# Layer 0's banded query operand in scratch padded to 32 rows and loaded once per unit; FFN heads and the second unit's load moved ahead of layer 1's weight products

## The chip, the cores and the metric

The kernel runs on one core of a Trainium2 chip. The metric is the device time of one execution in microseconds (us), here the median over several runs of the same program. The engines are TensorE (PE, with its weight loads as PEld), VectorE (DVE), ScalarE (ACT), GpSimd (POOL) and SyncE (SP), which issues most of the DMAs. Each engine works through its own list of instructions in order and waits on semaphores for the others. DMAs are put on a queue by SP or ACT and carried out by 16 DMA engines.

## The reference, cut to what matters

The input is x, 16 batches of 512 tokens with 128 features. Two layers of "macaron" form follow each other: half an FFN, attention, half an FFN. Layer 1 has a mixture of experts in its FFN and a linear attention; the change touches only weight products of it that are made ahead. What the change is about is layer 0:

```python
x = x + 0.5 * L0_ffn(layernorm(x))          # fp4_linear: blocks of 16, quantised and scaled back
x = x + L0_attn(layernorm(x))
x = x + 0.5 * L0_ffn(layernorm(x))
...
# L0_attn, 16 heads of 8 features:
idx  = arange(s); dist = clip(idx[None, :] - idx[:, None], -64, 64) + 64
pe_k = rel_emb_k[dist]; pe_v = rel_emb_v[dist]
score = einsum('bhqd,bhkd->bhqk', q, k) + einsum('bhqd,qkd->bhqk', q, pe_k)
attn  = softmax(score)
ctx   = einsum('bhqk,bhkd->bhqd', attn, v) + einsum('bhqk,qkd->bhqd', attn, pe_v)
```

The second term of the score depends on the distance of query and key. Outside a band around the diagonal the distance is clipped, and the term is a constant per query and side; inside the band it needs a matmul of its own.

## The kernel before, in words

**Units.** Layer 0 works in units: unit u = 2b + half is one half (256 queries) of batch b, for all 16 heads. A unit has two passes over its scores. The first, `maxima`, makes 32 score tiles of 128 keys by 512 columns, takes the running maximum of each on DVE (`mx`, L341), and ends with `mn`, the negated maximum of every query and head (L352), which goes by way of DRAM (`MD`, L353) into row 28 of each group of the tile `BD` (L355). The second, `main`, makes the same 32 tiles again, now with the maximum taken off by the matmul itself, exponentiates them on ACT (`PT`, L369) and multiplies by the values.

**One score tile** (`scores`). Four matmuls take keys `KS` against `BD` (L263). If the tile touches the band, eight more take `ET`, shifted rows of the relative key embeddings, against `TQ`, the queries arranged by head and distance (L267). The contraction runs over 128 rows, in four groups of 32 of which 24 are used by `TQ`.

**From queries to BD and TQ.** `prep(b)` normalises the batch, multiplies by the q and k weights, and splits the results into two f16 parts (`qkhi`, `qklo`). The k part and the q part go to the DRAM scratches `KSd` and `QS` (L302), some bias rows to `QS` as well (L309). For the band, the q parts are spread into `HM`, a tile that is zero except for its own head's rows, and twelve DMAs of 128 KB write it to the DRAM scratch `QM` (L300): on ACT's queue for batch 0, on SP's for the others. `loadK(b)` brings KS back in eight DMAs (L315), `load(b, half)` brings BD in four (29 rows, 58 KB each, L329) and TQ in four (24 rows each, L330; again on ACT's queue for batch 0). BD and TQ have three buffers, used by turns by the units. Their unused rows are zeroed once, TQ's on POOL, BD's on DVE.

**FFN steps.** `head(b, h)` is the first FFN of half a batch, `tail(b, h)` the second, each 21 steps of normalising, quantising, two products and a third one. `head` of a new batch begins with the load of x (L476), and DVE's first step on it is `ln_st` (L55). A tail ends with the store of x to DRAM (X, L487), which frees the x buffer for a later load.

**Order.** `layer0` writes the order out in a prologue and then hands over to `interleave`, which takes steps from the units' generators by due times: `main` of a unit runs beside `maxima` of the next, `head` three batches ahead and `prep` two batches ahead. On top of this a scheduler of the language places instructions on each engine by its own estimates, so that the order on an engine follows the program's text only loosely. The prologue before the change, where `pA` and `wp` are pools:

```python
            run(prep(0)); run(prepV(0)); loads(0); run(mxs(0,0))
            FFN1.pre(s,wp,[...],w)
        big=c.enter_context(tc.tile_pool(name="big",bufs=3))
        loads(1); ffn2(head,1); run(prep(1)); run(part(14)); ffn2(head,2)
```

`FFN1.pre` prepares layer 1's expert weights: for each of eight experts it loads w1 and w2 (L567), transposes w1 on PE (L568), multiplies and stores the product `We`. `Attn0.__init__` sets up layer 0's constants: `padv` and `hk` (L205, L207) for the values' embeddings, `padk` and `ET` for the keys', the zero row of QS (`zr`, L244), and four fills of KS on ACT (L236). The FFN's constructor quantises its weights and transposes them (L98) before head 0 can multiply.

Of the kernel before, what the change touches and what calls it, by code (L numbers as in the profile page):

```python
# [9 lines left out]
F16 = mybir.dt.float16  # L10
# [131 lines left out]
def f16split(nc, src, hi, lo, eng_lo):  # L142
    nc.vector.tensor_copy(hi,src)
    eng_lo.tensor_tensor(lo,src,hi,ALU.subtract)

class Attn0:

    def __init__(a, s, wk, pp, wqkv, bqkv, wout, bout, rek, rev):
        nc=s.nc; a.s=s; a.nc=nc
        c=s.const; dr=s.dram  # L150
# [70 lines left out]
        a.KS=[c.tile([128,2,2048],F16,name=f"a0_KS{i}") for i in range(2)]  # L221
        a.V=[c.tile([128,6,168],F32,name=f"a0_V{i}") for i in range(2)]
        a.cr=[c.tile([128,1024],F32,name=f"a0_cr{i}") for i in range(1)]
        for i in range(3): nc.vector.memset(a.BD[i],0.0); nc.gpsimd.memset(a.TQ[i],0.0)
        for t in a.V:
            nc.gpsimd.memset(t[:,:,144:168],0.0)
            nc.gpsimd.memset(t[:,:,0:144].rearrange("p w (h c) -> p w h c",c=9)[:,:,:,8:9],1.0)
# [8 lines left out]
            for sd in range(2): nc.scalar.activation(t[:,sd,:],a.BD[2].rearrange("p g h q -> p (g h q)")[:,0:2048],AF.Identity,bias=rm[:,sd:sd+1])  # L236
        zr=wk.tile([16,512],F16,name="zr"); nc.vector.memset(zr,0.0)
        a.QS=[dr.tile([16,29,512],F16,name=f"QS{i}") for i in range(2)]
        a.QM=[dr.tile([4,16,24,512],F16,name=f"QM{i}") for i in range(2)]
        a.KSd=[dr.tile([16,24,512],F16,name=f"KSd{i}") for i in range(2)]  # L240
        a.MD=[dr.tile([16,256],F16,name=f"MD{i}") for i in range(2)]
        a.X=4*8*1024+1024
# [32 lines left out]
    def prep(a, b, xb, wk, pM):  # L275
        s=a.s; nc=a.nc
        i=b%2
        QS=a.QS[i]; KSd=a.KSd[i]
        xn=wk.tile([128,4,128],F32,name="xn")
        yield from s.ln_steps(xb,xn,wk,4)  # L280
        ps=pM.tile([128,512],F32,name="mps")
        for j in range(4): nc.tensor.transpose(ps[:,j*128:(j+1)*128],xn[:,j,:],a.ident)
        xnT=a.xnT[b]=wk.tile([128,512],F32,name="xnT",bufs=2); nc.scalar.copy(xnT,ps); yield
        for z in range(2):
            ps=pM.tile([128,512],F32,name="mps")
            nc.tensor.matmul(ps,a.w[:,z*128:(z+1)*128],xnT,start=True,stop=True)
            f=wk.tile([128,512],F32,name="qk0") if z==0 else wk.tile([128,4,128],F32,name="xn").rearrange("p a b -> p (a b)")
            if z==0:
                for hf in range(2):
                    c=slice(hf*256,hf*256+256)  # L290
                    nc.scalar.activation(f[:,c].rearrange("p (b x j) -> p b j x",j=4,x=8),ps[:,c].rearrange("p (b j x) -> p b j x",j=4,x=8),AF.Identity,bias=a.bq[:,0:1],scale=float(1/np.sqrt(8.0)))
                q=f
            else: nc.scalar.activation(f,ps,AF.Identity,bias=a.bq[:,1:2])
            hi=wk.tile([128,512],F16,name="qkhi",bufs=2); lo=wk.tile([128,512],F16,name="qklo")
            f16split(nc,f,hi,lo,nc.gpsimd)
            if z==0:
                for t,e,m in ((hi,nc.vector,a.HM[0]),(lo,nc.gpsimd,a.HM[1])):
                    e.tensor_copy(bass.AP(tensor=m.tensor,offset=m.offset,ap=[m.ap[0],[513,4],[4,128]]),t.rearrange("p (y j) -> p j y",j=4))
                for p,t in enumerate((a.HM[0],a.HM[1],a.HM[0])):
                    for j in range(4): (nc.sync if b else nc.scalar).dma_start(a.QM[i][j][:,p*8:p*8+8,:],t[:,j,:])  # L300
            for p,t in enumerate((hi,lo,hi) if z==0 else (hi,hi,lo)):
                nc.sync.dma_start((QS,KSd)[z][:,p*8:p*8+8,:],t)  # L302
            yield
        ps=pM.tile([128,512],F32,name="mps")
        nc.tensor.matmul(ps[:32],a.eb.rearrange("p a b -> p (a b)"),q,start=True,stop=True)
        rhi=wk.tile([128,512],F16,name="qkhi",bufs=2)[:32]; rlo=wk.tile([128,512],F16,name="qklo")[:32]
        nc.vector.tensor_copy(rhi,ps[:32]); nc.vector.tensor_tensor(rlo,ps[:32],rhi,ALU.subtract)
        for sd in range(2):
            nc.sync.dma_start(QS[:,24+2*sd,:],rhi[16*sd:16*sd+16]); nc.sync.dma_start(QS[:,25+2*sd,:],rlo[16*sd:16*sd+16])  # L309
        yield  # L310
# [14 lines left out]
    def load(a, b, half):  # L325
        nc=a.nc; i=b%2
        u=(2*b+half)%3; BD=a.BD[u]; TQ=a.TQ[u]; QS=a.QS[i]
        for j in range(4):
            nc.sync.dma_start(BD[j*32:j*32+29,:,j,:],QS.rearrange("(g j) r q -> j r g q",j=4)[j][:,:,half*256:half*256+256])  # L329
            (nc.sync if b else nc.scalar).dma_start(TQ[j*32:j*32+24],a.QM[i][j][:,:,half*256:half*256+256].rearrange("h r q -> r h q"))  # L330

    def maxima(a, b, half, wk, pS, pM):

# [113 lines left out]
def interleave(*gens):  # L447

    live=[[g,n,0,f,t] for g,n,f,t in (q if len(q)==4 else (*q,0,1) for q in gens)]
    while live:  # L450
        k=min(live,key=lambda r:r[3]+(r[4]-r[3])*r[2]/r[1])
        try: next(k[0]); k[2]+=1
        except StopIteration: live.remove(k)
# [4 lines left out]
def layer0(tc, s, w, src, dst, nb=16):  # L458
    nc=tc.nc
    tok=lambda x,b: x[b].rearrange("(t p) d -> p t d",p=128)  # L460
    P="L0_attn_"; names=["W_qkv","b_qkv","W_out","b_out","rel_emb_k","rel_emb_v"]
    with ExitStack() as c:
        s.const=c.enter_context(tc.tile_pool(name="c",bufs=1))
        pM=c.enter_context(tc.tile_pool(name="pM",bufs=2,space=PS))
        pF=c.enter_context(tc.tile_pool(name="pF",bufs=0,space=PS)) if 0 else pM
        pS=c.enter_context(tc.tile_pool(name="pS",bufs=3,space=PS))
        pX=pS
        pA=c.enter_context(tc.tile_pool(name="pA",bufs=1,space=PS))
        wk=c.enter_context(tc.tile_pool(name="wk",bufs=1))
        fk=c.enter_context(tc.tile_pool(name="fk",bufs=2))  # L470
        xk=c.enter_context(tc.tile_pool(name="xk",bufs=5))
        X={}
        def xload(b):
            if b in X or b>=nb: return
            t=xk.tile([128,4,128],F32,name="x"); X[b]=t
            nc.sync.dma_start(t,tok(src,b))  # L476
        def head(b,h):

            if b<nb: xload(b); yield from F.half(X[b],h,fk,pF)
        def prep(b):  # L480
            if b<nb: yield from A.prep(b,X[b],wk,pM)
        def prepV(b):
            if b<nb: yield from A.prepV(b,pM)
        def tail(b,h):
            if b<0: return
            yield from F.half(X[b],h,fk,pF)
            nc.sync.dma_start(tok(dst,b)[:,2*h:2*h+2,:],X[b][:,2*h:2*h+2,:])  # L487
        def mxs(b,half):
            if b>=nb: return
            yield from A.maxima(b,half,wk,pX,pM)  # L490
        def loads(u):
            if u<2*nb:
                if u%2==0: A.loadK(u//2)
                A.load(u//2,u%2)
        def stream():
            for u in range(1,2*nb):
                for k,_ in enumerate(mxs(u//2,u%2)):
                    if k==16: loads(u+1)
                    yield
        st=stream()  # L500
        def part(n):
            for _ in range(n):
                if next(st,0)==0: return
                yield
        pl,hl=2,3
        W=dict(part=0,V=(.6,.7),fin=(.45,.9),prep=(0,.7),tail=1.0,head=(-.1,1))
        with tc.tile_pool(name="wp",bufs=1) as wp:
            for b in range(3): xload(b)
            F=FFN(s,w["L0_ffn_w_gate"],w["L0_ffn_w_up"],w["L0_ffn_w_down"],wp,pF)
            ffn2=lambda f,b: interleave((f(b,0),21,0,.8),(f(b,1),21,.2,1))  # L510
            ffn2(head,0)
            A=Attn0(s,wp,pS,*[w[P+n] for n in names])
            def run(g):
                for _ in g: pass
            run(prep(0)); run(prepV(0)); loads(0); run(mxs(0,0))
            FFN1.pre(s,wp,[pA.tile([128,512],F32,name=f"av{z}") for z in range(2)]+[pA.tile([128,512],F32,name="rps")],w)
        big=c.enter_context(tc.tile_pool(name="big",bufs=3))
        loads(1); ffn2(head,1); run(prep(1)); run(part(14)); ffn2(head,2)
        S=[(part(99999),33*2*nb,W['part'],2*nb+W['part'])]
        for b in range(nb):  # L520
            for h in range(2):
                u=2*b+h
                def at(g,n,f,t): S.append((g,n,u+f,u+t))
                at(A.main(b,h,X,wk,big,pS,pA,pM),59,0,1)
                fn,tl=(W['fin'],W['tail']) if u<2*nb-2 else ((.3,.5),.6)
                at(A.fin(b,h,X,wk,pM),5,1+fn[0],1+fn[1])
                at(tail(b,h),21,1+fn[1]+.001,1+fn[1]+tl)
                if b+hl<nb: at(head(b+hl,h),21,*W['head'])
                if h==0 and b+pl<nb: at(prep(b+pl),11,*W['prep'])
                if h==1 and b+1<nb: at(prepV(b+1),1,*W['V'])  # L530
        interleave(*S)
# [507 lines left out]
```

## Time and profile before

| | before |
|---|---|
| median of 3 runs | 3653.02 us (3648.55 to 3656.99) |
| the profiled execution | 3669.38 us, span 3667.4 us |
| mean granted TensorE clock | 0.90 |
| busy PE / DVE / ACT / POOL | 2895.4 / 2453.7 / 1702.8 / 839.6 us |
| first QS write issued | 86.15 us |
| first score matmul | 124.3 us |
| MD of units 0, 1, 2, 3 issued | 164.5, 219.9, 284.8, 345.1 us |
| layer 0 ends, about | 2095 us |

The times of the three runs and the profiled execution are of the same program; the profiled one was 16.4 us above the median. "Idle before, releaser" and the waits name what an engine stood waiting for, inferred from semaphores. The granted clock is the share of TensorE's full clock that it was allowed, and the DMA share is the mean over 16 DMA engines.

### The profile page before, as it was taken

To read this page: it belongs to the slowest core of one execution; us is meant where nothing else is said; L and a number is where in the kernel's file an instruction comes from. 1 tells how busy PE (TensorE), PEld (TensorE's weight loads), DVE (VectorE), ACT (ScalarE), POOL (GpSimd) and SP (SyncE) were. 2 spreads that over 40 slices of the span, in tenths; PEclk is the share of its full clock that TensorE was granted. 3 is DMA by queue.
4 is the path that set the end of the run, shared out by engine and by line. 5 is a ranking of instruction groups with operands and counts; after the bars stand their busy time and mean duration, and the time that the engine had idled before them with its cause. 6 is when DMAs were issued, how large, how long until landed. Compare 5 with 4: busy or idle time off the path is not lost. (4 is left out here: it accounts for less than half of the span.)

```text
span 3667.4 us, 95252 instructions
## 1 busy us (share of the span) xinstructions
PE 2895.4 (79%) x40077; PEld 2076.7 (57%) x40077; DVE 2453.7 (67%) x6508; ACT 1702.8 (46%) x3391; POOL 839.6 (23%) x789
## 2 busy tenths in 40 slices
PE   5579888898988989899988278882688888878570
PEld 3357666777767776677776144441465555555340
DVE  5568678777877788777764457774546656545357
ACT  3145445544554545545545155542455455445242
POOL 4122122222222222222101222222112121111226
PEclk8789999999999999999999588885899999999785
DMA  3232122322232122322210101104322222121301
GB/s 109 52 86 70 46 63 59 78 64 47 55 78 71 45 63 64 77 63 45 68 38 20 40 24 35 38 30 110 90 73 58 59 65 67 36 61 36 123 19 46
DMA packets 290159, 217.23 MB, mean 59 GB/s; under 512 B 77402, under 2 KB 257476, under 8 KB 289604
## 3 DMA queue, kind: packets, MB, share of 16 engines
q1 hardware_dynamic: 284468, 207.72, 21.5%
q8 instruction: 315, 5.16, 0.6%
q10 hardware_dynamic: 5264, 3.43, 0.4%
q14 instruction: 112, 0.92, 0.1%
HBM read 110.28 MB, written 100.78 MB: 58 GB/s over the span
## 5 line engine op out<-in xcount | busy, mean ns | idle before, releaser
L341 DVE TRANSPOSE_TENSOR_REDUCE mx<-sps 128x16 f32<-128x512 f32 x1024 | 706.0, 701 | 262.3 <-PE sps L267 138.6
L263 PE MATMUL sps<-a_BD,a_KS 128*128 128x128 f16 x8192 | 745.5, 222 | 156.2 <-DVE mx L341 96.2
L369 ACT ACTIVATE PT<-sps 128x512 f32<-128x512 f32 x1024 | 580.4, 598 | 554.0 <-PE sps L267 289.1
L263 PEld LDWEIGHTS <-a_KS 128*128 128x128 f16 x8192 | 540.3, 98 | 309.2 <-issue 257.7
L59 POOL TENSOR_TENSOR ln_rs<-ln_ve,negh 128x4 f32<-128x4 f32 (+1 forms) x192 | 175.3, 921 | 857.1 <-DVE ln_ve L58 778.3
L267 PE MATMUL sps<-a_TQ,a_ET 128*128 128x64 f16 x7168 | 370.2, 194 | 0.3 <-issue 0.3
L722 DVE SCALAR_TENSOR_TENSOR moe<-mps,oh,moe 128x128 f32<-128x128 f32 x896 | 289.8, 341 | 112.7 <-PE mps L720 99.7
L79 POOL TENSOR_TENSOR q_M<-q_y,q_M 128x704 f32<-128x704 f32 (+2 forms) x129 | 159.2, 1235 | 862.4 <-DVE q_y L78 650.7
L720 PE MATMUL mps<-f_W,T 128*128 128x512 f32 x512 | 302.9, 714 | 17.9 <-DVE moe L722 13.6
L267 PEld LDWEIGHTS <-a_ET 128*128 128x128 f16 x7168 | 309.8, 99 | 6.9 <-issue 6.5
L274 PE MATMUL av<-PT,a_V 128*32 128x256 f32 x3840 | 251.4, 386 | 0.0
L895 DVE TENSOR_TENSOR a_at<-pp,a_cm 128x1024 f32<-128x1024 f32 x128 | 154.4, 1215 | 71.7 <-PE pp L893 71.0
L274 PE MATMUL rps<-PT,a_TV 128*32 128x64 f32 x6912 | 199.5, 225 | 0.1
L893 PE MATMUL pp<-a_F 64*128 64x128 f32 x2048 | 165.1, 300 | 37.6 <-DVE a_at L895 29.9
L893 PEld LDWEIGHTS pp<-a_F 64*128 64x128 f32 x2048 | 139.3, 201 | 84.1 <-DVE a_at L895 36.0
L720 PEld LDWEIGHTS mps<-f_W,T 128*128 128x128 f32 x512 | 104.4, 227 | 118.5 <-issue 75.0
L274 PEld LDWEIGHTS av<-PT,a_V 128*32 128x32 f32 x3840 | 135.4, 111 | 55.8 <-issue 1.9
L274 PEld LDWEIGHTS rps<-PT,a_TV 128*32 128x32 f32 x6912 | 129.7, 110 | 50.1 <-issue 26.1
L875 ACT ACTIVATE a_F<-pp 128x1024 f32<-128x1024 f32 x128 | 127.0, 1027 | 45.5 <-PE pp L873 30.5
L62 ACT ACTIVATE xn<-xn,ln_mr,ln_rs 128x128 f32<-128x128 f32 x256 | 103.7, 483 | 87.8 <-DVE ln_mr L60 44.3
L139 PE MATMUL mps<-wdT,hT 128*128 128x128 f32 (+1 forms) x768 | 134.0, 313 | 7.6 <-ACT hT L136 7.3
L674 ACT COPY f_PT<-St 32x512 f32<-32x512 f32 x128 | 78.7, 615 | 105.4 <-DVE St L673 101.3
(342 smaller groups left out, 5338.3 us busy)
## 6 DMA issues: line engine op xcount, KB each, us to landing
QM<-a_HM SPq DMA_DIRECT2D x180, 128.0 KB
a_TQ<-QM SPq DMA_DIRECT2D x120, 192.0 KB
RD<-RV SPq DMA_DIRECT2D x32, 512.0 KB
a_KS<-KSd SPq DMA_DIRECT2D x128, 96.0 KB
a_QK<-a1d SPq DMA_DIRECT2D x128, 96.0 KB
xn<-X SPq DMA_DIRECT2D x32, 256.0 KB
a1d<-a_hi SPq DMA_DIRECT2D x64, 128.0 KB
a_BD<-QS SPq DMA_DIRECT2D x128, 58.0 KB
```

The costliest lines, as they stand in the source:

```text
L59: nc.gpsimd.tensor_tensor(rs,ve,s.negh[:,:n],ALU.pow); yield
L79: nc.gpsimd.tensor_tensor(M[:P],y[:P],M[:P],ALU.subtract)
L139: nc.tensor.matmul(ps[:,384:512],hT[:P,c,:],f.wdT[:P,c,:],start=(c==0),stop=(c==2),skip_group_check=True)
L263: nc.tensor.matmul(o4[:,g],KS[:,sd,g*512+kt*128:g*512+(kt+1)*128],BD[:,g,:,b*32:b*32+32].rearrange("p h (x j) -> p x h j",j=4),start=(g==0 ...
L267: nc.tensor.matmul(out[:,x*64:x*64+64],a.ET[:,w0:w0+128],TQ[:,:,b*32+4*x:b*32+4*x+4],start=False,stop=(x==7),skip_group_check=True)
L274: for p,q in mms[1:]: a.nc.tensor.matmul(*p,**q)
L341: r=nc.vector.tensor_reduce(mx[:,kt,:,bb],ps.rearrange("p (i c) -> p i c",c=32),axis=AX.X,op=ALU.max,apply_transpose=True)
L369: nc.scalar.activation(pt[:,:,bb*32:bb*32+32].rearrange("p h (x j) -> p x h j",j=4),ps.rearrange("p (x h j) -> p x h j",x=8,j=4),AF.Exp)
L720: nc.tensor.matmul(ps,yT[:,j*128:(j+1)*128],a.W[:,e2*4:e2*4+4,:],start=True,stop=True)
L722: nc.vector.scalar_tensor_tensor(moe[:,j,:],ps[:,e*128:(e+1)*128],oh[:,j,e2*4+e:e2*4+e+1],moe[:,j,:],ALU.mult,ALU.add)
L893: nc.tensor.matmul(ps[:,hh,bs],f[hh*64:hh*64+64,1,bs],f[hh*64:hh*64+64,0,bs],start=True,stop=True)
L895: nc.vector.tensor_tensor(k,ps.rearrange("p h (b q) -> p (h b) q",b=4),a.cm.unsqueeze(1).to_broadcast([128,8,128]),ALU.mult)
```

## The change

The scratch QM is laid out anew: by half of the batch, by group, then 32 rows (24 of data and 8 that stay zero), heads and 256 queries, so that a unit's TQ tile lies in DRAM as it stands in SBUF, 128 rows of 8 KB. Sixteen DMAs in the setup write the zero rows, from HM while it is all zero. The three memsets of TQ on POOL go. Each batch writes QM in 24 DMAs of 64 KB instead of 12 of 128 KB, behind the QS writes in the text and on SP's queue for every batch, and `load` fetches TQ in one DMA of 1 MB instead of four of 192 KB, on SP for every batch, ahead of BD's four. In `layer0`, the line with the second unit's loads, head 1, prep 1, fourteen steps of maxima and head 2 moves in front of `FFN1.pre`, into the block of the pool `wp`.

```diff
-        for i in range(3): nc.vector.memset(a.BD[i],0.0); nc.gpsimd.memset(a.TQ[i],0.0)
+        for i in range(3): nc.vector.memset(a.BD[i],0.0)
...
-        a.QM=[dr.tile([4,16,24,512],F16,name=f"QM{i}") for i in range(2)]
+        a.QM=[dr.tile([2,4,32,16,256],F16,name=f"QM{i}") for i in range(2)]
+        for i,t in enumerate(a.QM):
+            for k in range(8): nc.sync.dma_start(t[k//4,k%4,24:32].rearrange("r (c h) q -> (r c) (h q)",c=2),a.HM[i].rearrange("p j q -> p (j q)")[k*16:k*16+16])
...
-                for p,t in enumerate((a.HM[0],a.HM[1],a.HM[0])):
-                    for j in range(4): (nc.sync if b else nc.scalar).dma_start(a.QM[i][j][:,p*8:p*8+8,:],t[:,j,:])
             for p,t in enumerate((hi,lo,hi) if z==0 else (hi,hi,lo)):
                 nc.sync.dma_start((QS,KSd)[z][:,p*8:p*8+8,:],t)
+            if z==0:
+                for hf in range(2):
+                    for p,t in enumerate((a.HM[0],a.HM[1],a.HM[0])):
+                        for j in range(4): nc.sync.dma_start(a.QM[i][hf,j,p*8:p*8+8].rearrange("r h q -> h r q"),t[:,j,hf*256:hf*256+256])
...
+        nc.sync.dma_start(TQ,a.QM[i][half].rearrange("j r h q -> (j r) h q"))
         for j in range(4):
             nc.sync.dma_start(BD[j*32:j*32+29,:,j,:],QS.rearrange("(g j) r q -> j r g q",j=4)[j][:,:,half*256:half*256+256])
-            (nc.sync if b else nc.scalar).dma_start(TQ[j*32:j*32+24],a.QM[i][j][:,:,half*256:half*256+256].rearrange("h r q -> r h q"))
...
-            run(prep(0)); run(prepV(0)); loads(0); run(mxs(0,0))
+            run(prep(0)); run(prepV(0)); loads(0); run(mxs(0,0)); loads(1); ffn2(head,1); run(prep(1)); run(part(14)); ffn2(head,2)
             FFN1.pre(s,wp,[pA.tile([128,512],F32,name=f"av{z}") for z in range(2)]+[pA.tile([128,512],F32,name="rps")],w)
         big=c.enter_context(tc.tile_pool(name="big",bufs=3))
-        loads(1); ffn2(head,1); run(prep(1)); run(part(14)); ffn2(head,2)
```

## The prediction

> **What bounds the kernel now.** First the page: TensorE is busiest, and layer 0's two big consumers are the score matmuls and VectorE's running maxima.
>
> ```profile
> PE 2895.4 (79%) x40077; PEld 2076.7 (57%) x40077; DVE 2453.7 (67%) x6508; ACT 1702.8 (46%) x3391; POOL 839.6 (23%) x789
> ...
> L341 DVE TRANSPOSE_TENSOR_REDUCE mx<-sps 128x16 f32<-128x512 f32 x1024 | 706.0, 701 | 262.3 <-PE sps L267 138.6
> ...
> QM<-a_HM SPq DMA_DIRECT2D x180, 128.0 KB
> a_TQ<-QM SPq DMA_DIRECT2D x120, 192.0 KB
> ...
> a_BD<-QS SPq DMA_DIRECT2D x128, 58.0 KB
> ```
>
> An average says nothing of the prologue, so next the table by stretches, cut at the first QS write (86.15), the first score (124.3) and the issue of MD (the negated maxima) of units 0 to 3. Columns: start and end, length, busy PE, PEld, DVE, ACT, POOL, then granted clock, DMA share, GB/s.
>
> ```profile
> 86.15:124.30 38.15, 6.17 (x16) 2.57 (x17) 5.22 (x8) 1.52 (x3) 4.15 (x3) 0.54 0.56 132
> 124.30:164.50 40.20, 29.19 (x309) 24.05 (x310) 37.82 (x85) 5.55 (x16) 10.35 (x10) 0.77 0.02 7
> 164.50:219.90 55.40, 44.23 (x724) 32.84 (x721) 40.80 (x82) 20.97 (x46) 11.75 (x10) 0.95 0.33 79
> 219.90:284.80 64.90, 51.71 (x784) 38.84 (x785) 40.22 (x82) 30.55 (x64) 13.68 (x13) 0.88 0.26 65
> 284.80:345.10 60.30, 56.36 (x1040) 43.56 (x1033) 48.38 (x109) 30.57 (x68) 16.73 (x16) 1.00 0.31 84
> 345.10:2095.00 1749.90, 1520.24 (x26261) 1196.83 (x26259) 1301.35 (x2886) 853.20 (x1855) 382.55 (x363) 0.95 0.23 57
> ```
>
> For 38 us nearly everything stands (PE 6.17, DVE 5.22); in the next 40 us DVE is full (37.82 of 40.20). The waits between 86.15 and 220 say why (total, times, longest):
>
> ```profile
> PE sps L263 <- DMA a_BD<-QS: 20.2, 2, 15.7
> ACT f_x L116 <- DMA a_TQ<-QM: 18.6, 1, 18.6
> DVE mx L341 <- PE sps L267: 21.5, 4, 16.2
> ```
>
> The first scores wait for BD. ACT, which issues batch 0's QM writes and TQ loads itself, cannot start head 1's copy f_x for 18.6 us, and head 1 then shares DVE with the first maxima. Last, the waits of the steady part, 330 to 2050:
>
> ```profile
> PE sps L263 <- DVE mx L341: 75.6, 107, 4.6
> ...
> DVE ln_st L55 <- DMA x<-in_L_attn_x_dram: 43.4, 11, 8.0
> ...
> PE sps L263 <- DMA a_BD<-MD: 0.6, 1, 0.6
> ```
>
> PE works 1520 of those 1720 us. It never waits for MD's way back; but DVE waits for the x load in eleven batches, and PE's own gaps around these waits add up to 36.8 us. So x is on the path, MD has room.
>
> **Setup (up to the first QS write).** The three TQ memsets leave POOL: 10.4 us between 5.7 and 16.1, in which one small DVE step took 2.40 us instead of 0.19. ACT's four KS fills move to the front, so the quantised-weight transposes (40.59) can start about 2 us earlier. Against it SP gets 16 pad writes of 64 KB between padv and hk. The trace has none; the nearest rows, writes of 16 rows, take 0.30 to 0.56 us to issue, a QM write 0.61: 5 to 10 us of SP, mostly while it waited for work. Pushed back: hk (issued 25.86) and the first w1t (19.28 to about 34). The weight products then no longer stand ahead of the quantised-weight transposes but among head 0's steps: the instruction order has about one expert there instead of five. I put the first QS write at 84, between 81 and 91.
>
> **First QS write to first score: 38.2 us before.** Queue SP, in the new order: QS x3, QM x24, KSd x3, QS rows, TQ, KS x8, BD x4. Before, batch 0's 12 QM writes and 8 TQ loads ran on ACT's queue beside it; so here all of the QM time is new in SP's line. A QM write took 0.61 to 0.65 us with 128 rows; the new ones have 128 rows too, of half the size, so I take the same: the second batch, which had its 12 on SP already, needed 39.3 us from QS to landed BD. From that: +12 x 0.65 = +7.8. TQ becomes one issue instead of three in front of BD (-2.0), and a 1.2 us wait for a qklo write is covered: about 43. The 1 MB TQ load (128 rows of 8 KB) has hk as its row: packets of 342 to 367 ns, 8 for each of 16 engines, 2.9 us, against 8 TQ loads before (3072 packets of 42 ns, 8 us of all engines) which shared the engines with the KS loads; the KS loads should lose less. Bounds 40 and 48; first score at 84 + 43 = 127 (+2.7; with the setup's bounds -3 and +15). BD itself stays: 4 x 3.03 us, one load's 116 packets of 29 ns after another at a DMA share of 0.07, one engine's worth.
>
> The Trainium skill ("DMA: Bandwidth & Descriptors", "Issuing engines are not separate DMA queues") says that issuing on several engines saves only sequencer time, usually small beside the transfer. By that, moving QM from ACT to SP would be about free and the first score would come at about 119. The rows speak otherwise: the issue is the longer part here, 0.61 us against 128 packets of 55 ns spread over 16 engines, 0.44 us.
>
> **First score to first MD: 40.2 us before.** In the new order both halves of head 1 and most of head 2's first steps stand in front of the first scores on DVE, PE and ACT; ACT is free of DMA issues. Summed with the median durations of this trace, DVE's work from the first maximum to MD of unit 0 falls from 45.3 to 32.0; scaled by its real 40.2/45.3 that is 28.4 us. PE's work there hardly falls (107.6 to 105.8 in the same sum), its busy time was 29.2 at a clock of 0.77. So I take 30, bounds 28 and 35. The moved work finds 38 idle us: free, unless FFN's ACT or POOL steps are late there; if that cover is gone, its 13 us come back. MD of unit 0: 127 + 30 = 157, 7.5 earlier.
>
> **Units 1 to 3.** Same DVE work in sum by unit 3. Two stalls of PE, 4.5 us for BD of unit 2 at 217.6 and 1.9 us for MD at 174.5, should shrink, since batch 1's QS and QM now go ahead of MD of unit 0: -3.5 (0 to -6). MD of unit 3: 11 us earlier (bounds, all ends together, 21 earlier and 9 later).
>
> **Steady part.** (a) 12 more QM issues per batch, +7.8 us of SP, stand in front of MD of the odd units: from QS's first issue to the last KSd it is 12.0 to 14.2 us in batches 5 to 15, so 20 to 22 after; mn is ready 16.7 to 19.1 after QS, MD 2 to 4 us late. The first exponential of an odd unit comes 18 to 21 us after its mn, while BD's MD rows are issued by 9.4: some 8 us of room, so cost 0 (batch 4 alone, 10 late, may lose 2). RD and cr behind it have most of a unit. TQ saves six issues of 0.3 to 0.45 us a batch. (b) The x load. Before, SP issued X store, KS x3, x; x landed 5.2 to 7.0 us after the store, and 8.2 to 8.9 in the two batches with a BD load in front. After: X store, KS, TQ (1 MB), BD, x: so 8 to 10, +2.4 to +4. But DVE's ln_st now stands 5 maxima behind the step that frees the store, not 3; 2 maxima are 1.4 us (2 x 0.70, busy) to 3.7 (2 of 32 in 59 us). Between -1.3 and +2.6 a batch, x 11 x 36.8/43.4: -12 to +24; I take 0, the middle of both spans. Layer 1 keeps its order.
>
> **Sum.** 3669.4 (the profiled execution; span 3667.4 and 2.0 around it) - 7.5 - 3.5 = 3658. That execution lay 16.4 us above the median, so the median becomes 3653.0 - 11 = 3642. A change under 0.2%, 7.3 us, this kernel's measurement cannot tell from none (its three runs span 8.4).
>
> **Rivals.**
> *The x load takes it all back and more (slower).* Place: ring order behind TQ and a one-engine BD load, before ln_st. Price: 2.6 us x 11 x 0.85 = 24 us, 3666 in all. It decides once x lands more than about 1.5 us later than the two extra maxima last. For: the two batches with BD in front waited 8.0 and 5.0 us; against: the order moved ln_st back. 0.20.
> *Nothing to see.* 24 QM issues on one queue push the first score to +8 and half-clock scores keep 35 us: MD of unit 0 at 167, the later stalls shrink by 3: 3653. For: the clock was 0.54 before the first scores. 0.17.
> *Larger gain.* First score in time, 28 us to MD, stalls gone (-20), and x's wait shrinks (-12): 3621. For: TQ's small packets go, 1536 a unit to 128. 0.15.
> *MD of odd units eats its room* (slower): were the 24 issues 1 us each, not 0.65, MD would be 3 + 8 = 11 late against 8 of room, 3 us in 14 batches, 3684. Against: no QM row shows it. 0.03.
> Forecast: 0.45, own range 3630 to 3652. The range for 8 in 10 reaches towards both sides: 3619 to 3668. Faster: 0.40 of the forecast and the larger gain, 0.55; same: 0.05 of the forecast and nearly all of the second rival, 0.21; slower: 0.24.
>
> **What would show it.** Right: ACT has no wait for TQ; PE and DVE are busier between QS and first score; first score near 127, MD of unit 0 near 157, of unit 3 near 334, and that lead kept to layer 1's start. Wrong: DVE's waits for x above 43 us with PE gaps to match; PE waiting for BD<-MD; first score after 132.

## The result, and the profile after

The changed kernel takes 3688.97 us (median of 4 runs, 3683.54 to 3693.26) against 3655.01 us for the kernel before in the same comparison (3648.55 to 3658.89): a ratio of 1.0094, 95% interval 1.0073 to 1.0115. It is 34 us slower, where 3642 and a range up to 3668 had been forecast. Its profiled execution has a span of 3685.8 us.

The table by stretches, cut where that of before was cut: first QS write, first score, MD of units 0, 1, 2, 3, end of layer 0.

```profile
83.40:126.70 43.30, 19.62 (x49) 8.61 (x50) 19.49 (x48) 5.96 (x15) 13.31 (x11) 0.58 0.46 128
126.70:157.00 30.30, 24.56 (x303) 19.30 (x303) 27.57 (x55) 5.78 (x14) 7.84 (x8) 0.89 0.12 32
157.00:205.80 48.80, 40.41 (x693) 32.73 (x691) 36.70 (x80) 17.77 (x42) 8.24 (x7) 0.95 0.31 81
205.80:275.50 69.70, 56.98 (x852) 42.42 (x851) 46.84 (x85) 31.09 (x62) 11.73 (x11) 0.91 0.24 65
275.50:337.10 61.60, 52.95 (x968) 39.77 (x968) 44.42 (x98) 28.95 (x64) 15.15 (x15) 0.95 0.34 86
337.10:2106.00 1768.90, 1523.87 (x26267) 1183.39 (x26264) 1289.28 (x2882) 851.40 (x1855) 385.29 (x363) 0.95 0.23 60
```

The prologue did what was forecast: the 43 us from QS to the first score hold 19 us of PE and DVE work instead of 6 and 5, and MD of unit 0 is issued at 157.0 instead of 164.5. MD of unit 3 is 8.0 us earlier than before (337.1 against 345.1). The last row is where it is lost: beside the last row of before it has the same number of matmuls to within 6, the same PE and DVE busy time to within 1%, and is 19 us longer. MD of unit 31 goes out at 1975.1 against 1964.1: from 8 us ahead to 11 us behind.

The waits of the steady part, 330 to 2050:

```profile
PE sps L265 <- DVE mx L345: 90.5, 79, 6.9
...
DVE ln_st L55 <- DMA x<-in_L_attn_x_dram: 74.2, 11, 7.7
```

In this stretch no line of PE waiting for BD<-MD is left, though MD of the odd units is now issued 4.3 to 6.1 us behind mn from unit 5 to 25. What grew is DVE's wait for x: eleven waits as before, 74.2 us instead of 43.4. Summed from the trace, PE's own gaps around these eleven places (from the wait's start to 5 us past its end) are 66.3 us instead of 36.9.

The last of these places in the time line of SP. Columns: start, time taken by the issues, instruction. First before, then after:

```profile
1602.58 0.39 SPq L487 DMA_DIRECT2D X<-x  x1
1603.02 2.50 SPq L315 DMA_DIRECT2D a_KS<-KSd  x3
1606.37 0.40 SPq L476 DMA_DIRECT2D x<-in_L_attn_x_dram  x1
1606.81 0.35 SPq L329 DMA_DIRECT2D a_BD<-QS  x1
```

```profile
1610.02 0.39 SPq L491 DMA_DIRECT2D X<-x  x1
1610.45 0.42 SPq L319 DMA_DIRECT2D a_KS<-KSd  x1
1610.98 0.35 SPq L332 DMA_DIRECT2D a_TQ<-QM  x1
1611.37 0.30 SPq L334 DMA_DIRECT2D a_BD<-QS  x1
1613.01 0.40 SPq L480 DMA_DIRECT2D x<-in_L_attn_x_dram  x1
```

x is issued 3.0 us after the store, no later than before (3.8 here). But it now has TQ's 1 MB and a BD load in front, and DVE goes on at 1619.7, 6.7 us after the issue instead of 3.0. The DMA view of the changed kernel between 1609 and 1622 shows what lies between, in 40 slices of 0.325 us:

```profile
DMA  6867679989979999998897400000000000000000
GB/s 224 218 230 173 145 202 244 172 205 284 303 262 318 388 403 403 429 454 328 279 340 214 118 27 20 20 19 20 19 20 19 19 19 20 19 20 19 20 20 19
```

TQ's 128 packets of 8 KB (312 ns in the median, the slowest 876) fill the engines up to about 1615.3, x's packets follow until 1616.5, and then packets come one after another at 20 GB/s, as from one engine: by my reading the one with BD's 116 packets and, behind them, the last share of x. In e3 below, where x has a queue of its own, its packets can be told from BD's.

### The profile page after: what moved, and what is told of

Read it like the earlier page. It is cut to its first block, busy times and chain, and to the rows that moved or that the text cites. A ratio compares the mean times of both kernels' runs of the same rounds, so it can differ in the third digit from the quotient of the medians.

```text
span 3685.8 us, 95390 instructions
## 1 busy us (share of the span) xinstructions
PE 2910.6 (79%) x40077; PEld 2068.0 (56%) x40077; DVE 2443.8 (66%) x6508; ACT 1701.5 (46%) x3391; POOL 831.0 (23%) x786
## 5 line engine op out<-in xcount | busy, mean ns | idle before, releaser
L276 PEld LDWEIGHTS av<-PT,a_V 128*32 128x32 f32 x3840 | 122.5, 110 | 63.6 <-issue 0.2
```

Source lines behind the costliest of these rows:

```text
L276: for p,q in mms[1:]: a.nc.tensor.matmul(*p,**q)
```

## The experiments

In these later comparisons, made on four chips (e0 to e3, e4 to e7, e8 to e10, e11), the kernel before ran at 3678 to 3684 us instead of 3655; every ratio is taken within its own comparison. "Waits" are DVE's for x, "gaps" PE's around them, in us as above; MD are issue times.

| kernel | first score | MD 0 | MD 3 | MD 31 | waits | gaps | ratio (95%) |
|---|---|---|---|---|---|---|---|
| before, first trace | 124.3 | 164.5 | 345.1 | 1964.1 | 43.4 | 36.9 | 1 |
| e0 before, again | 127.3 | 167.4 | 346.9 | 1970.4 | 43.3 | 36.9 | |
| changed | 126.7 | 157.0 | 337.1 | 1975.1 | 74.2 | 66.3 | 1.0094 (1.0073 to 1.0115) |
| e1 line moved only | 125.9 | 166.1 | 350.3 | 1973.8 | 45.7 | 38.3 | 1.0008 (0.9987 to 1.0028) |
| e2 layout only | 127.3 | 157.4 | 336.0 | 1993.8 | 86.8 | 78.8 | 1.0081 (1.0056 to 1.0107) |
| e3 x on ACT's queue | 130.7 | 159.9 | 339.4 | 1984.1 | 75.1 | 67.3 | 1.0045 (1.0028 to 1.0063) |
| e4 batch 0 on SP | 125.9 | 158.4 | 324.9 | 1951.8 | 48.4 | 42.0 | 0.9949 (0.9928 to 0.9969) |
| e5 heads later | 125.1 | 154.3 | 329.5 | 1909.5 | 34.1 | 29.8 | 0.9867 (0.9843 to 0.9891) |
| e6 BD 32 rows | 114.9 | 144.4 | 312.5 | 1942.2 | 77.3 | 69.4 | 0.9940 (0.9918 to 0.9963) |
| e7 TQ behind BD | 126.4 | 156.6 | 338.5 | 1991.5 | 89.0 | 87.4 | 1.0053 (1.0037 to 1.0070) |
| e11 both e6 and e7 | 116.4 | 145.6 | 312.2 | 1904.4 | 46.7 | 45.1 | 0.9834 (0.9801 to 0.9867) |
| e8 both e5 and e6 | 112.0 | 141.5 | 305.5 | 1844.8 | 35.0 | 30.7 | 0.9681 (0.9653 to 0.9709) |
| e9 as e8, no padding | 113.5 | 144.0 | 315.9 | 1858.8 | 34.8 | 30.3 | 0.9728 (0.9701 to 0.9756) |
| e10 e4 and heads later | 127.7 | 159.1 | 322.4 | 1874.8 | 34.8 | 31.1 | 0.9734 (0.9707 to 0.9761) |

### e1 and e2: which half of the change costs, which gains

e1, of before:

```diff
-            run(prep(0)); run(prepV(0)); loads(0); run(mxs(0,0))
+            run(prep(0)); run(prepV(0)); loads(0); run(mxs(0,0)); loads(1); ffn2(head,1); run(prep(1)); run(part(14)); ffn2(head,2)
...
-        loads(1); ffn2(head,1); run(prep(1)); run(part(14)); ffn2(head,2)
```

> The kernel before with only the line of the prologue moved (second unit's loads, head 1, prep 1, 14 steps, head 2 ahead of the weight products); QM, TQ and the queues as before. Theory X (the loss is the x load, queued on SP behind the 1 MB TQ load and a one-engine BD load): the order at the x load is that of before (KS x3 ahead in nine of eleven batches), so DVE's waits for x stay near 43 us and TensorE's gaps around them near 37; the prologue gain of 8 us stays: about 3646 against 3655. Theory M (the moved work, or what it does to layer 1, costs the time): 3675 or more. Theory Q (the 24 QM writes per batch on SP): as theory X here.

e2 is the changed kernel with this line back in its old place.

> The changed kernel with the prologue's line put back where it was; padded QM, 24 QM writes on SP and one TQ load per unit stay. Theories X and Q: the loss of the steady part is here, DVE waits for x about 74 us, TensorE's gaps there about 66; the prologue gain goes and the first score is late: 3690 to 3700. Theory M: close to before, 3655 to 3662.

All three theories missed part of this. The loss is in the layout (e2 1.0081), as theories X and Q had it. But the prologue's gain is there too: MD of unit 0 at 157.4 in e2, at 166.1 in e1. The moved line does nothing: the lists of instructions of e1 and of before are the same on all five engines, and so are those of e2 and the changed kernel. The scheduler had put both texts into one order. So e1 and e2 are also second samples of the two kernels, and they show how far two profiles of the same order can differ: MD of unit 31 at 1975.1 (changed) and 1993.8 (e2). A difference of less than some 19 us between two single traces is thus not clear of chance.

### e0: the kernel before, profiled again

> The kernel before, unchanged, profiled once more: its first profiled execution was 16 us above the median of its runs. If the excess is chance between executions, this one's span is 3645 to 3660, and the shift of layer 1 against the changed kernel (+7 us in the first pair of traces) comes out otherwise; if the profiler adds it, the span is again near 3667.

The span is 3681.4 us, in neither range, since the whole comparison ran 23 us longer than the first. The execution, 3683.3, lies 5 us above its median (3678.3), among 19 runs that span 27 us. So the first profile of before, some 14 us above its runs' median of 3655.0, was most likely high by chance; the two first profiles differ by 18 us and the medians by 34. Of the 14.0 us between the two profiles of the same kernel, 6.4 arise before MD of unit 31 and 7.6 after it. The 7.4 us that the changed kernel lost after that point in the first pair can't be told from this.

### e4: where the prologue's gain comes from

```diff
-                    for j in range(4): (nc.sync if b else nc.scalar).dma_start(a.QM[i][j][:,p*8:p*8+8,:],t[:,j,:])
+                    for j in range(4): nc.sync.dma_start(a.QM[i][j][:,p*8:p*8+8,:],t[:,j,:])
...
-            (nc.sync if b else nc.scalar).dma_start(TQ[...],...)
+            nc.sync.dma_start(TQ[...],...)
```

> The kernel before with one edit: batch 0's 12 QM writes and 8 TQ loads go on SP's queue like those of the other batches; no padding, no move of a line. Theory A (the prologue's gain comes from ACT, which no longer issues these DMAs and runs on with head 1): first score at 127 to 131, MD of unit 0 at 156 to 161 against 167, and the lead stays, since the order at the x load is that of before in most batches: time 5 to 12 us below before. Theory L (the gain needs the single TQ load): first score 135 or later, MD of unit 0 at 165 or later, no gain or a loss of up to 5 us.

Theory A holds, with more than it asked: 0.9949, 18.5 us below before. ACT, free of 20 DMA issues that took it 18.1 us in e0, does head 1's copies at 94.5 and 104.9 where they were at 107.9 and 132.9 (e0), and the head fills the stretch from QS to the first score: DVE works 17.1 us there instead of 5.2. ACT's wait for TQ is gone; what is left of its waits at this copy, from 89.7 to 220:

```profile
ACT f_x L116 <- PE mps L115: 9.5, 3, 4.1
```

Neither padding nor one TQ load is needed. At MD of unit 3 e4 is 22 us ahead of e0, the changed kernel only 10: in the changed kernel DVE waited 7.5 us for a cr load (until 259.6), a wait that e4 does not show.

e4 and e2 share the gain at MD of unit 0 (158.4 and 157.4) and differ in the layout and what it does to the order. At MD of unit 31 they are 42.0 us apart: 11.1 of it has come by unit 3, and 30.9 from there, where PE's gaps at x alone differ by 78.8 - 42.0 = 36.8.

### e3: x on another queue

```diff
-            nc.sync.dma_start(t,tok(src,b))
+            nc.scalar.dma_start(t,tok(src,b))
```

> The changed kernel with one edit: the x loads are issued by ACT, so they stand in another queue's rings than TQ and BD; everything else on SP as in the changed kernel. Theory X: x lands 5 to 7 us after the X store instead of 9.5 to 11, DVE's waits for x fall from 74 to 25 to 45 us, TensorE's gaps from 66 to 20 to 40, and the time falls by 25 to 45: 3645 to 3664. Theory Q (SP's longer line delays MD, RD and cr): no change, 3684 to 3692. A third way: the DMA engines themselves are busy with TQ, and x is late on any queue: waits 60 or more, 3680 to 3690.

The third way: DVE went on 9.0 to 10.5 us after the store, against 9.5 to 11.0; waits 75.1. Theory X as put, that the place in the queue decides, fell: packet by packet, the x load issued at 1016.2 began at 1018.5, when TQ's 8 KB packets were ending (the last at 1019.4), on the other queue too. Its end shows the second load in front: from 1020.9 to 1021.7 packets of x and of SP's queue, 512 bytes each, take turns one by one, 27 to 36 ns apiece, as on a single engine. The Trainium skill ("DMA: Bandwidth & Descriptors", "Issuing engines are not separate DMA queues") says that DMAs of all engines run on the same 16 DMA engines and interleave; here the other queue gained 0.6 us (from issue to DVE's next step 6.4 us in the mean, against 7.1). The ratio fell by 0.4 to 0.5% against the changed kernel and e2, more than that explains; this stays open, as with e7. The same section prices the issue itself as usually small. Here the issues were not small: standing in ACT's line, their 18.1 us cost the prologue its cover, which e4 got back.

### e6, e7 and e11: the two loads in front of x, singly and together

e6 widens BD's loads (QS gets rows 29 to 31, zero):

```diff
-            nc.sync.dma_start(BD[j*32:j*32+29,:,j,:],QS...)
+            nc.sync.dma_start(BD[j*32:j*32+32,:,j,:],QS...)
```

e7 moves the line of the TQ load behind the loop of BD's loads. e11 does both.

> The changed kernel with BD's loads widened from 29 to 32 rows (QS with three more zero rows), which should spread a load over all engines instead of one. If BD's one-engine line is what holds x back: VectorE's waits for x fall from 74 to about 45; if TQ's 1 MB does: they stay above 65. In either case a BD load is issued in under 1 us instead of 3, the first score comes 8 to 10 us earlier (about 118). Time 8 to 35 us below the changed kernel: ratio to before 1.000 to 1.007.

> The changed kernel with the TQ load after the four BD loads in the text: on SP x then stands behind two BD loads, and TQ follows x. If TQ's 1 MB holds x back: VectorE's waits for x fall to 40 to 50 and the ratio to before to 0.999 to 1.004; if the BD loads do: x still lands 9 to 11 us after the store, waits 65 to 90, ratio 1.006 to 1.011.

> The changed kernel with both edits that alone left x late: BD's loads of 32 rows, and the TQ load behind them. On SP the x load then stands behind one KS and two short BD loads, TQ behind x. Theory X (either of the two, TQ's 1 MB or a one-engine BD load, is enough to hold x back, so only both together free it): x lands 5.5 to 7.5 us after the store as before the change, VectorE's waits for x fall from 77 (BD 32 rows alone) and 89 (TQ behind alone) to 35 to 50, TensorE's gaps there from 69 and 87 to 30 to 45, and the ratio to before falls from 0.994 to 0.983 to 0.989. Theory Q (SP's longer line costs the steady part, and x only shows it): waits 65 or more, ratio 0.992 to 0.998.

In e7 two BD loads stand ahead of x and TQ behind it, in e6 TQ and one short BD load ahead. With either edit alone, x stays late: store to DVE's next step 9.8 us in e6 and 10.3 in e7, means over eleven batches, against 10.0 in the changed kernel and 6.8 before. With both it is 6.5. The three lines, e6, e7 and e11:

```profile
DVE ln_st L55 <- DMA x<-in_L_attn_x_dram: 77.3, 11, 8.4
```

```profile
DVE ln_st L55 <- DMA x<-in_L_attn_x_dram: 89.0, 11, 8.7
```

```profile
DVE ln_st L55 <- DMA x<-in_L_attn_x_dram: 46.7, 11, 5.3
```

e11's ratio, 0.9834, lies where theory X had put it, and theory Q's 0.992 to 0.998 is out. e7 and e11 put all but 325 of DVE's 6508 instructions in the same places, so between these two it is BD's width that frees x; from e6 to e11 the order changes too (1836 places). From e6 to e11 the gaps fall by 24 us and MD of unit 31 comes 38 us earlier; the 14 us beyond the gaps lie within the 19 by which two traces of one order differ, and these two are from different chips. In e7, e2, the changed kernel and e6 the granted clock in the 6 us from DVE's next step on is 0.50, 0.53, 0.56 and 0.57 in the mean over the eleven places, in e11, e0, e4 and before 0.67, 0.69, 0.70 and 0.74.

The ratios of e6 and e7, 0.9940 and 1.0053, lie below what had been expected with x late (1.000 to 1.007 and 1.006 to 1.011). e6 also gains in the prologue, 12 us at the first score. SP's time line has the four BD loads of unit 0 in the changed kernel and in e6:

```profile
111.18 8.29 SPq L334 DMA_DIRECT2D a_BD<-QS  x4
```

```profile
109.83 1.77 SPq L335 DMA_DIRECT2D a_BD<-QS  x4
```

The Trainium skill ("DMA: Bandwidth & Descriptors", "Why a DMA increments its semaphore by 16 and not by 1") lets a DMA use the largest number up to 16 that divides the slowest dimension of both sides. 29 rows leave one engine, 32 rows all 16; the traces agree: with 29 rows 18 to 20 GB/s from 115 to 120 and 8.29 us for the four issues, with 32 rows 137 GB/s and more between 109.5 and 112.5, and 1.77 us.

### e5, e8, e9 and e10: heads due later, with and without padding

```diff
-        W=dict(...,head=(-.1,1))
+        W=dict(...,head=(.05,1))
```

> The changed kernel with one number changed: heads fall due 0.05 of a unit after the unit's start instead of 0.1 before it. On SP the x load then stands behind three KS loads and ahead of TQ and BD; VectorE's first step on x is 2 maxima behind the step before the store. Theory X (x behind TQ and BD costs the time): x lands 5 to 7 us after the store, VectorE's waits for x 40 to 55 instead of 74 to 87, TensorE's gaps there 35 to 50 instead of 66 to 79: about 30 us less than the changed kernel, ratio to before 0.997 to 1.003. Theory Q (24 QM writes on SP, late MD, RD and cr): ratio 1.007 to 1.011 as for the changed kernel.

> The changed kernel with both edits: heads due at 0.05, and BD loaded with 32 rows. If the two gains are independent (x's place in the steady part, the BD loads in the prologue), the prologue's 10 to 13 us of the second come on top of the first: MD of unit 0 near 143, VectorE's waits for x near 34, ratio to before 0.982 to 0.985. If the BD loads only mattered while x stood behind them: 0.986 to 0.988.

> The kernel before with batch 0's DMAs on SP, heads due at 0.05 and BD loaded with 32 rows: all the edits that helped, without the padded QM, the 24 writes and the single TQ load. If the padded layout is worth nothing by itself, the ratio is that of the kernel with padding and the same edits, within 0.2%; if the single TQ load pays once x no longer stands behind it, this one is 0.3% or more slower; if the 24 writes cost, it is 0.3% or more faster.

> The kernel before with batch 0's DMAs on SP and heads due at 0.05, without padding and with BD's loads of 29 rows. If the later heads gain only by x's place behind TQ, they gain little here, where x stood behind KS loads already (waits 48): ratio 0.992 to 0.995. If they gain by the order of the other steps too: 0.982 to 0.989.

e5 gained far more than x explains: waits 34.1, gaps 29.8, 49 less than e2, but MD of unit 31 84 us earlier. e10 shows why e5 is no proof for x: without padding, where x stood behind KS loads in most batches, later heads gain as well, from 0.9949 to 0.9734, more than the 0.982 expected at best. How they do so I have not taken apart. With later heads and BD's 29 rows the padded kernel is still 1.3% slower than the unpadded one (e5 against e10). In e5 DVE waits 26.6 us for the KSd write of qklo, which stands behind the 24 QM writes on SP, and e10 has no such wait among its longest: theory Q's place, argued from the trace and not tried by itself; e8, the fastest, still has 18.1 us of it. With BD's 32 rows the padded layout is ahead (e8 against e9, 0.9681 against 0.9728), as expected if the single TQ load pays once x is out of its way. Without padding BD's 32 rows gain nothing that can be measured (e9 0.9728, e10 0.9734), though the first score comes 14 us earlier: the traces have that lead up to MD of unit 31, and e9 needs 18 us more from there to the end, which stays open. The gains of e5 and e6 were more than independent: 0.982 to 0.985 had been expected. e8 beats both kernels, 117 to 120 us below before.

## Why the prediction was wrong

**The prologue's times held, its reason did not.** First QS write 83.4 (forecast 84), first score 126.7 (127), MD of unit 0 157.0 (157), QM writes 0.60 us each (0.65). But I gave the filled stretch to the moved line as much as to ACT. The order of the whole change had been set against that of before, not that of its two halves; the moved line changes no instruction's place, and e4 gets the filled stretch without it.

**Units 1 to 3** brought 0.5 us instead of 3.5, so that MD of unit 3 was 8.0 us earlier instead of 11: of the stalls named, 4.5 and 1.9 us, 1.1 is left, and DVE's 7.5 us for cr, with 9.0 us of PE behind it, came in their place.

**Odd units' MD**: late by 4.3 to 6.1 (forecast 2 to 4), and the room of 8 us held it. First exponentials came 19 to 22 us after mn.

**The step that failed is (b), the x load.** I had its place, its mechanism and its rival, and set it to 0 as the middle of both spans. That was a slip: the middle of -1.3 and +2.6 a batch is +0.65, that of -12 and +24 is +6 us. I had also passed over a third late batch of before, 8.8 us after the store with only KS loads in front (the store at 890.9). Landing, taken as DVE's next step, was +3.2 us in the mean (6.8 to 10.0 after the store; bounds 2.4 and 4). What I got wrong is the counterweight. Two more maxima should have kept DVE busy 1.4 to 3.7 us; from the end of the step that frees the store to DVE's stop it was 4.8 us before and 5.5 after, 0.7 more. That is below my lower bound, since that stretch is not paced by DVE's own steps: in nine of the eleven batches of before it holds three maxima in 4.7 us, in the changed kernel five (once four) and three short steps in 5.5, in e11 five maxima in 4.8. So the wait grew by 2.8 us a batch, and PE's gaps by 29.4 us, beyond the rival's 24: the sign that I had named for being wrong, DVE's waits for x above 43 us with PE gaps to match. A second term may have been missing, the clock behind the gap. The tables by stretches around the place above, before and after:

```profile
1605.80:1609.40 3.60, 2.61 (x91) 2.28 (x91) 0.12 (x2) 1.08 (x5) 0.00 (x0) 1.00 0.39 115
1609.40:1614.00 4.60, 3.10 (x26) 2.87 (x26) 4.60 (x20) 0.63 (x3) 1.12 (x2) 0.63 0.22 59
```

```profile
1613.50:1619.70 6.20, 1.86 (x54) 1.59 (x52) 0.01 (x1) 1.40 (x6) 0.00 (x0) 0.89 0.47 167
1619.70:1625.00 5.30, 4.16 (x44) 4.09 (x44) 4.23 (x17) 0.60 (x1) 1.36 (x2) 0.50 0.07 20
```

In the first rows of each, DVE (third busy time) stands and PE runs dry; in the second PE starts again, at a clock of 0.50 after the longer gap. 6 us at 0.56 instead of 0.69 to 0.74 (the two traces of before) are, as an estimate, about 1 us of full clock a batch; no run shows it as time.

**The sum.** In the first pair of traces it is -8.0 to unit 3, +19 from there to unit 31 (of it +29.4 at x; what gives some 10 back I have not found) and +7.4 after it, 18.4 in all. By the medians it is 34; the rest is that the profile of before lay 14 us above its median and that of the changed kernel 1 below. With the other traces of the same two orders (e0 and e1; e2) the means part by -10.9 to unit 3, +26 from there to unit 31 (gaps at x +35) and -0.8 after it. So the likeliest single term of the forecast was off by 29 us of PE gaps in the first pair and by 42 in e2 against before, of which 19 and 39 show as time between unit 3 and unit 31; and the range, which let in x's bound of 24 beside a full prologue gain, ended 21 us short. That x is the largest part of the loss is shown by the gaps and by e11; how the 34 us divide to the last is not.

## What to carry to other kernels

Where a transfer has room only because it happens to stand behind small ones, look at what a change puts in front of it in the transfers' order: a single large load (e6) and two loads that only one DMA engine can carry (e7) were each enough to hold it back. When work in front of a waiting instruction is to hide a delay, measure how long the engine takes from the release to its stop, not the sum of the durations in between. And take the order of instructions for each part of a change by itself, before giving a part the credit.

## What the runs showed of the hardware that I had not expected

Another issuing queue gave the x load only 0.6 us: once 1 MB in 8 KB packets was under way, x waited for it from ACT's queue as from SP's. And a PE gap of 5 to 7 us has a low clock behind it (0.50 to 0.64 over the next 6 us at all eleven places of the changed kernel; 0.50 to 1.00 before, where most gaps were of 2 to 3 us). In the means it goes from 0.77 in e5, with gaps of 29.8 us in all, to 0.50 in e7 with 87.4. That such a gap costs more time than its length is not shown: in the first pair the time grew by less than the gaps. The Trainium skill ("TensorE: Matmul & The Clock Gate", "Part 1: The HAM clock gate") has the clock fall to half after an idle stretch and rise after some sustained work; the rows agree, and no run here shows the threshold.
